# A two-layer attention and expert kernel: the projection bias of two row tiles is added in memory by accumulating transfers, and row loads, row sums and counts move

## The chip, the cores and the metric

The kernel runs on one core of one Trainium2 chip. The metric is the device time of one launch in microseconds (us), lower is better. Three runs of the kernel before gave 1204.27, 1204.51 and 1206.26 us; their median is 1204.51 us.

## The reference

The input x has 4 x 16 x 16 positions of 1024 channels, that is 1024 rows of 1024 float32 values. The kernel's tiles of rows are numbered 0 to 7, 128 rows each, two for each of the four images.

```python
# layer 0: group norm, q, k and v projections, content and position terms
x = x + _L0_conv_ref(_gn(x), Wq, Wk, Wv, ...)
# layer 1, attention: 16 heads of 64, causal, over 256 positions of each image
t = _to_tokens(x)
att = softmax(causal(q @ k.T / 8));  y = att @ v
t = t + (y @ W_proj.T + b_proj)
# layer 1, experts: 8 experts of 1024 x 1024, weights under 0.1 dropped
w = softmax(n @ gate_w + gate_b);  w = w * (w >= 0.1);  w = w / sum(w)
t = t + sum_e w[:, e] * (n @ expert_w[e] + expert_b[e])   # n = _ln_t(t)
```

What the change touches is `t + (... + b_proj)`: the rows after layer 0, the bias of the attention's output projection, and the product with `W_proj`. It also touches the bookkeeping of the experts: which rows have a weight of at least 0.1 for an expert, and how many such rows stand in the tiles before.

## The kernel before, in words

All work is on 128-row tiles in float32. A product of 128 x 1024 by 1024 x 512 is eight matmuls, which show as sixteen matmul records; many products are done as blocks by a Strassen-like scheme with seven products of four matmuls (eight records) each, whose operand sums are made on VectorE. `manual_schedule` blocks fix the order of the instructions of each engine as they are written; between two such blocks a scheduler merges what is ready.

**Layer 0** ends with a loop over the eight tiles (lines 636 to 660). The order of tiles is t = 1, 3, 5, 7, 0, 2, 4, 6. For the first six, GpSimd adds the broadcast bias `b_proj` to the rows (L647) and stores them to `x_rows` in memory (L656). The last two, t = 4 and t = 6, are stored by SyncE without the bias (L658 and L660).

**Attention** is a loop over d = 0 to 17 (L1028). In a step, TensorE does a few projection products (L682), multiplies the softmaxed scores of step d-2 with the values (L911, tile `pa`), and makes the scores of step d (L842). The scores of a step take a way through memory: `scored` scales them on GpSimd (L883), SyncE stores them (L889) and reads them back in four parts by quarters (L893, tile `s_rows`), and `turn_back` transposes them on VectorE (L898, tile `s_T`). There are two such sets, one after the other, in each step. SyncE works its queue in order, so a read back that waits holds up what is queued behind it. The weights of the next head pairs (`load_qk`, L785) are on that same queue at d = 0, 4 and 8.

From d = 13 the rows come back from memory. `load_x(t)` (L1051) is a 512 KB transfer on GpSimd's queue into `xs[t]`: t = 0 at d = 13, t = 1, 2 and 3 during d = 14, t = 4 and 6 in d = 15, t = 5 and 7 in d = 16. At the start of d = 15 the bias is loaded too, broadcast over 128 partitions (`bp`, L1084), and at d = 17 GpSimd adds it to tiles 4 and 6 (L1103). Tiles 2 and 3 (b = 1) are the first pair whose output projection goes by `product_out(1, n, ...)` (L964). `sum_of_weights(n)` (L947) makes its operand sums of the weights, `row_sums_out(b)` (L960) those of the rows. At the end of d = 16 `sum_of_weights(4)` stands ahead of `turn_back(17)`.

**The rest of the output projection** is a second `manual_schedule` block (L1545). TensorE does `product_out(1, 4)`, then the seven products of tiles 4 and 5 (b = 2, the second pair that goes by the seven-product scheme), then the full products of tiles 6 and 7. After each matmul `one_more` (L1538) counts one chunk, and the table `at_chunk` (L1487) says which stages of the gating are issued there, as pairs (stage, tile): 0 normalises a finished tile and stores it to `rows`, from where SyncE reads it back by quarters (L1276 and L182); 1 transposes it (L187); 2 is the product with the gate weights (L1325, tile `parts`); 3 and 4 are the softmax (`gate`) and the cut at 0.1 (`thresholds`); 5 counts rows per expert (`place`: L1380 adds the tile's kept flags to the running count `kept`, L1382 and L1383 turn flags and counts into positions on TensorE); 6 and 7 enter the rows into the experts' lists. Tiles 0 to 2 are gated together, and tiles 3 to 5. The table `others` (L1525) places single actions, among them `row_sums_out(2)` at chunk 12.

At chunk 8 tiles 0 and 1 are normalised; at chunk 12 tile 2 is normalised and then come the row sums of b = 2, so on VectorE the four sums (L160 to L163) stand behind the normalisation of tile 2. The transposes of tiles 0, 1 and 2 are issued at chunks 16, 20 and 26 and the product with the gate weights at chunk 30.

The experts' part (from L1588) takes the last 470 us and is not changed.

Of the kernel before, what the change touches and what calls it, by code (L numbers as in the profile page):

```python
# [32 lines left out]
F32 = mybir.dt.float32  # L33
I32 = mybir.dt.int32
AF = mybir.ActivationFunctionType
ALU = mybir.AluOpType
# [3 lines left out]
P = 128  # L40
C = 1024
# [4 lines left out]
NT = TOK // P  # L46
# [23 lines left out]
def kernel(  # L70
# [27 lines left out]
    nc = tc.nc  # L98

    def pool(stack, name, bufs=1, **kw):  # L100
        return stack.enter_context(tc.tile_pool(name=name, bufs=bufs, reuse_waits="tile", **kw))
# [49 lines left out]
    x_rows = dram.tile([TOK, C], F32, name="x_rows")  # L151
# [71 lines left out]
            nc.scalar.copy(dst[:, 4 * j : 4 * j + 4, ts(t, P)], pt.rearrange("p (c n) -> p c n", c=4))  # L223


    in_order, bp_home = ExitStack(), ExitStack()
    with ExitStack() as layer0:
        l0 = pool(layer0, "l0")
        xn = x_pool.tile([P, NC, TOK], F32, tag="x", name="xn")
# [434 lines left out]
    with ExitStack() as attention:  # L664
# [295 lines left out]
        def row_sums_out(b):  # L960
            a, s = rows_out_of(b)
            sums_of_A(*a, *s)
# [64 lines left out]
        with tc.manual_schedule():  # L1027
            for d in range(len(doubles) + lag):  # L1028
                if d % 4 == 0 and d < 12:
                    load_qk(d // 4 + 1)  # L1030
                elif d == 12:
                    w_p.append(w_tile("w_p0", W_projT[:, :HALF]))

                def values_and_scores(at):
                    if at >= lag:
                        values(at - lag, turned_s.pop(at - lag))
                    if at < len(doubles):
                        made[at] = scores(at)

                def go_on(at, between=lambda: None):  # L1040
                    if at - 1 in made:
                        first_one, second_one = made.pop(at - 1)
                        soft[at - 1] = [scored(*first_one)]
                        between()
                        soft[at - 1].append(scored(*second_one))

                def turn_back(at):
                    if at >= lag:
                        turned_s[at - lag] = [turned(*one) for one in soft.pop(at - lag)]

                def load_x(*some):  # L1051
                    for t in some:
                        nc.gpsimd.dma_start(xs[t], x_rows[ts(t, P), :])

                ahead = units.get(d, ())
                if d < 14:
                    for unit in ahead[:1]:
                        project_qk(*unit)
                    turn_back(d)
                    go_on(d)  # L1060
                    for unit in ahead[1:]:
                        project_qk(*unit)
                    if d == 13:
                        sums.close()
                        x_pool = pool(x_home, "xb", side="right")
                        xs = [x_pool.tile([P, C], F32, tag=f"x{t}", name=f"xb{t}") for t in range(NT)]
                        bp = pool(bp_home, "bp", side="right").tile([P, C], F32, tag="bp", name="bp")
                        load_x(0)
                    values_and_scores(d)
                elif d == 14:  # L1070
                    project_qk(*ahead[0])
                    go_on(14, lambda: load_x(1))
                    project_qk(*ahead[1])
                    turn_back(14)
                    w_p.append(w_tile("w_p1", W_projT[:, HALF:]))
                    sums_out.append(big_tile(1, "sums_out", (4 * Q, HALF)))
                    load_x(2)
                    project_out(*outs[14][0], {NC - 3: lambda: values_and_scores(14)}, True)
                    turn_back(15)
                    project_out(*outs[14][1], {}, True)  # L1080
                    go_on(15)
                    load_x(3)
                elif d == 15:
                    nc.gpsimd.dma_start(bp, b_proj.partition_broadcast(P))  # L1084
                    product_out(1, 1, tr)
                    product_out(1, 2, tr, {1: lambda: values_and_scores(15)})
                    sum_of_weights(1)
                    sum_of_weights(2)
                    project_out(*outs[15], {NC - 1: lambda: go_on(16)}, True)
                    row_sums_out(1)  # L1090
                    load_x(4, 6)
                    turn_back(16)
                elif d == 16:
                    project_out(*outs[16], {}, True)
                    load_x(5, 7)
                    product_out(1, 6, mm)
                    sum_of_weights(3)
                    product_out(1, 5, mm, {1: lambda: values_and_scores(16)})
                    sum_of_weights(4)
                    turn_back(17)  # L1100
                else:
                    for b, nt in tiles[NT - 2 :]:
                        nc.gpsimd.tensor_add(xs[2 * b + nt], xs[2 * b + nt], bp)  # L1103
                    product_out(1, 3, tr)
                    product_out(1, 7, tr, {1: lambda: values_and_scores(17)})
        share_banks("ps_rest", 3)
        bp_home.close()


    left.close()  # L1110
# [91 lines left out]
    with ExitStack() as gating:  # L1202
# [149 lines left out]
            nc.scalar.activation(weight, weight, AF.Exp)  # L1352
            return weight, top, keep

        def thresholds(weight, top, keep):
            n = top.shape[1]
            all_of = top.unsqueeze(2).to_broadcast([P, n, E])
            if n > 1:
                nc.vector.tensor_reduce(top, weight, AX.X, ALU.add)
            nc.vector.reciprocal(top, top)  # L1360
            if n == 1:
                of = weight[:, 0, :]
                nc.vector.tensor_scalar(keep[:, 0, :], of, top, THRESHOLD, ALU.mult, ALU.is_ge)
                nc.vector.scalar_tensor_tensor(of, of, top, keep[:, 0, :], ALU.mult, ALU.mult)
            else:
                nc.vector.tensor_mul(weight, weight, all_of)
                nc.vector.tensor_scalar(keep, weight, THRESHOLD, None, ALU.is_ge)
                nc.vector.tensor_mul(weight, weight, keep)
            nc.vector.tensor_reduce(top, weight, AX.X, ALU.add)
            nc.vector.scalar_tensor_tensor(top, top, 0.0, top, ALU.is_equal, ALU.add)  # L1370
            nc.vector.reciprocal(top, top)
            nc.vector.tensor_mul(weight, weight, all_of)
            return keep

        def place(tiles, keep):


            n, t0 = len(tiles), tiles[0]
            for i, t in enumerate(tiles):
                nc.vector.tensor_add(kept[:, t + 1, :], kept[:, t, :], keep[:, i, :])  # L1380
            pp = tr(f"pp{t0}")[:, : n * E]
            nc.tensor.matmul(pp, before, keep.rearrange("p n e -> p (n e)"), start=True, stop=False)  # L1382
            nc.tensor.matmul(  # L1383
                pp, ones, kept[:, t0 : t0 + n, :].rearrange("p n e -> p (n e)"), start=False, stop=True
            )
            slot = of_tiles("place", n, E)
            nc.vector.scalar_tensor_tensor(slot, keep, 0.0, from_end[:, t0 : t0 + n, :], ALU.is_equal, ALU.mult)
            at = l2w.tile([P, 3, n, E], I32, tag="at", name=f"at{t0}", padded_shape=[P, 3, 3, E])
            nc.vector.tensor_add(at[:, 0, :, :], slot, pp.rearrange("p (n e) -> p n e", n=n))
            nc.vector.tensor_scalar(at[:, 1, :, :], at[:, 0, :, :], 31, None, ALU.bitwise_and)  # L1390
            nc.vector.tensor_scalar(at[:, 2, :, :], at[:, 0, :, :], 5, None, ALU.logical_shift_right)
            return at
# [74 lines left out]
        def stage(n, t):  # L1467
            tiles = together[t]
            if n == 0:
                normal[t] = normalise(t)  # L1470
            elif n == 1:
                turned_rows[t] = turn_rows(t, normal[t])
            elif n == 2:
                summed[t] = gate_sums(tiles)
            elif n == 3:
                gated[t] = gate(tiles, summed[t])
            elif n == 4:
                gated[t] = thresholds(*gated[t])
            elif n == 5:
                placed[t] = place(tiles, gated[t])  # L1480
            elif n == 6:
                entered[t] = entries_of(t, t - tiles[0], placed[tiles[0]])
            else:
                enter(t, *entered[t])
# [16 lines left out]
            47: ((7, 1),),  # L1501
            48: ((1, 4),),
            50: ((7, 2),),
            53: ((1, 5),),
            55: ((2, 3),),
            57: ((0, 6),),
            58: ((3, 3),),
            59: ((4, 3),),
# [11 lines left out]
        def load_table(function):  # L1520
# [2 lines left out]
            nc.scalar.activation(of, ident[:, 0:1], function)  # L1523

        others = {  # L1525
            12: lambda: row_sums_out(2),
            29: lambda: nc.gpsimd.dma_start(
                w_p[1][:, : NC // 2, :], W_projT[:HALF, HALF:].rearrange("(c p) n -> p c n", p=P)
            ),
# [447 lines left out]
```

## Time and profile before

| | |
|---|---|
| median of three runs | 1204.51 us |
| the profiled execution | 1204.73 us |
| its span, first to last instruction | 1202.9 us |
| TensorE busy | 1191.1 us (99% of the span) |
| VectorE busy | 799.0 us (66%) |
| GpSimd busy | 416.2 us (35%) |
| ScalarE busy | 211.2 us (18%) |
| granted TensorE clock | 1.0 |

The span is the time from the first to the last instruction on the engines of the profiled execution; 1.8 us of the 1204.73 us lie around it. Times in the timelines count from the start of the span. A line of a timeline has the start, the duration (of a group: from its first start to its last end), the engine, the line in the kernel, the operation, what it writes and reads, shapes and how many; in square brackets how long the engine stood idle before it and what ended that. A line of the chain of waits has the start, the duration and the step that the work waited for. PE is TensorE, DVE VectorE, ACT ScalarE, POOL GpSimd and SPq SyncE's queue.

Attention runs from about 358 us to 650 us, the rest of the output projection to about 723 us, and the experts from there.

### The profile page before, as it was taken

The numbers are of one execution on the slowest core, as the hardware profiler recorded it, in microseconds if no ns is written. First come the engines' busy times: TensorE is split into PE (matmuls) and PEld (weight loads), VectorE is DVE, ScalarE is ACT, GpSimd is POOL, SyncE is SP. The second block draws the span as 40 slices with busy tenths as digits, with TensorE's granted clock in tenths as the row PEclk, the third lists the DMA queues.
The fourth block names the chain that finished last, engine by engine and source line by source line (L and its number), as shares of the span: only waits on it lengthen the run. The fifth ranks groups of instructions, "written<-read, shape, count | busy, mean of one in ns | idle before, by whom it ended". The sixth has DMA issues, their size and how long they took to land.

```text
span 1202.9 us, 13637 instructions
## 1 busy us (share of the span) xinstructions
PE 1191.1 (99%) x4866; PEld 649.3 (54%) x4866; DVE 799.0 (66%) x1394; ACT 211.2 (18%) x523; POOL 416.2 (35%) x470
## 2 busy tenths in 40 slices
PE   9999999999999999999999999999999999999998
PEld 5444884788884444444544464454344435444544
DVE  5796736678332666566679867897677767667852
ACT  3310111130001222122221212111111111111111
POOL 1051351365000122222333116546474554555411
PEclk9999999999999999999999999999999999999999
DMA  9102014882201353535565777484757475666434
GB/s 348 35 1 70 19 41 112 273 277 69 70 9 62 102 174 109 163 93 167 164 199 181 228 245 242 101 234 113 223 121 220 100 241 130 189 145 198 77 62 72
DMA packets 94330, 170.83 MB, mean 142 GB/s; under 512 B 12048, under 2 KB 49440, under 8 KB 94256
## 3 DMA queue, kind: packets, MB, share of 16 engines
q1 hardware_dynamic: 72880, 105.08, 26.6%
q0 software_dynamic: 16960, 54.59, 19.1%
q10 hardware_dynamic: 4416, 10.22, 2.4%
q8 instruction: 40, 0.66, 0.2%
q14 instruction: 34, 0.28, 0.1%
HBM read 117.17 MB, written 48.50 MB: 138 GB/s over the span
## 4 chain that ended last, share of the span: by engine, by line
PE 93%; DVE 3%; DMA 2%; issue 1%; SPq 0%; ACT 0%; POOL 0%; DVEq 0%; POOLq 0%
PE p L1662 27%; PE pqk L682 15%; PE pv L682 8%; PE joint L1724 4%; PE pq_pair L413 4%; PE pq L328 4%; PE left L1769 3%; PE po L1006 3%; PE pT L525 3%; PE py L617 2%; PE pk L444 2%; PE pc L465 2%; PE pv L553 2%; PE sc L842 2%; PE rest L1783 2%; PE pa L911 2%
## 5 line engine op out<-in xcount | busy, mean ns | idle before, releaser
L1145 POOL DMA_INDIRECT w_e_xg<-rows,gather x146 | 164.3, 1125 | 54.2 <-issue 42.4
L1662 PE MATMUL p<-w_e,A 128*128 128x512 f32 x368 | 162.1, 593 | 0.0
L883 POOL TENSOR_TENSOR s_q<-s_q,total 128x128 f32<-128x128 f32 (+1 forms) x128 | 61.8, 518 | 275.3 <-DVE total L880 264.4
L1662 PEld LDWEIGHTS p<-w_e,A 128*128 128x128 f32 x368 | 69.6, 190 | 86.8 <-issue 85.9
L1168 POOL DMA_INDIRECT out_dram<-y,add x32 | 58.7, 1834 | 163.6 <-issue 78.6
L1662 PE MATMUL p<-T,S 128*128 128x512 f32 x256 | 112.7, 592 | 0.0
L1711 ACT ACTIVATE y<-y,slot 128x512 f32<-128x512 f32 x64 | 45.4, 721 | 318.1 <-DVE y L1676 146.6
L682 PE MATMUL pqk<-ln,w_qk 128*128 128x512 f32 x192 | 85.7, 595 | 0.0
L1662 PEld LDWEIGHTS p<-T,S 128*128 128x128 f32 x256 | 48.6, 190 | 60.8 <-issue 60.3
L868 ACT ACTIVATE s_q<-sc,top 128x128 f32<-128x128 f32 (+1 forms) x128 | 52.0, 419 | 156.4 <-DVE top L864 137.8
L682 PEld LDWEIGHTS pqk<-ln,w_qk 128*128 128x128 f32 x192 | 36.1, 190 | 43.7 <-issue 42.1
L682 PE MATMUL pqk<-T,S_qk 128*128 128x512 f32 x128 | 57.8, 595 | 0.0
L1662 PE MATMUL p<-w_e,S 128*128 128x512 f32 x128 | 57.5, 592 | 0.0
L1006 PE MATMUL po<-w_p,y_T 128*128 128x512 f32 x112 | 50.7, 599 | 0.0
L328 PE MATMUL pq<-w_q,xn 128*128 128x512 f32 x96 | 44.5, 599 | 0.3 <-ACT xn L308 0.3
L682 PE MATMUL pv<-w_v,ln 128*128 128x256 f32 x192 | 43.2, 379 | 0.0
L1769 PE MATMUL left<-w_e,one 128*32 128x512 f32 x312 | 41.8, 593 | 0.0
L1662 PEld LDWEIGHTS p<-w_e,S 128*128 128x128 f32 x128 | 24.3, 190 | 30.6 <-issue 28.9
L898 DVE STREAM_TRANSPOSE s_T<-s_rows 128x768 f32<-128x768 f32 x32 | 30.2, 962 | 15.9 <-DMA s_rows<-s_rows 15.7
L187 DVE STREAM_TRANSPOSE A<-w_e_xg 128x1024 f32<-128x1024 f32 x32 | 39.5, 1235 | 1.4 <-DMA w_e_xg<-rows,gather 1.3
L682 PEld LDWEIGHTS pqk<-T,S_qk 128*128 128x128 f32 x128 | 24.0, 190 | 29.2 <-issue 27.7
L682 PEld LDWEIGHTS pv<-w_v,ln 128*128 128x128 f32 x192 | 36.4, 190 | 4.9
(388 smaller groups left out, 2056.0 us busy)
## 6 DMA issues: line engine op xcount, KB each, us to landing
w_e<-in_expert_w_dram SPq DMA_DIRECT2D x13, 2048.0 KB, 11.4
s_rows<-s_q SPq DMA_DIRECT2D x32, 384.0 KB, 2.3
s_rows<-s_rows SPq DMA_DIRECT2D x128, 96.0 KB, 2.4
w_qk<-in_W_attnT_dram SPq DMA_DIRECT2D x8, 1024.0 KB, 5.7
w_e<-in_expert_w_dram ACTq DMA_DIRECT2D x3, 2048.0 KB, 11.2
w_q<-in_Wq_dram SPq DMA_DIRECT2D x16, 256.0 KB, 6.8
x_at<-in_x_dram POOLq DMA_DIRECT2D x8, 512.0 KB
w_p<-in_W_projT_dram SPq DMA_DIRECT2D x2, 2048.0 KB, 8.3
```

Source lines behind the costliest of these rows:

```text
L328: nc.tensor.matmul(pq, xn[:, c, ts(t, P)], w_q[kc][:, c, :], start=(c == 0), stop=(c == NC - 1))
L413: nc.tensor.matmul(bank, a[:, c, :], b[:, c, :], start=(c == 0), stop=(c == NC // 2 - 1))
L682: nc.tensor.matmul(bank, stationary(c), moving(c), start=(c == 0), stop=(c == NC // 2 - 1))
L868: nc.scalar.activation(blocks(h, qt), psc[:, h, cols].rearrange("p (b f i) -> p b f i", f=Q, i=32), AF.Exp, bias=top[:, qt, h : h + 1], sc ...
L883: nc.gpsimd.tensor_mul(blocks(h, qt), blocks(h, qt), total[:, qt, h : h + 1].unsqueeze(2).unsqueeze(3).to_broadcast([P, 1 + qt, Q, 32]),)
L1006: nc.tensor.matmul(po, y_T[:, c, ts(t, P)], w_p[j][:, c, :], start=(c == 0), stop=(c == NC - 1))
L1145: nc.gpsimd.indirect_dma_start(out=row[:, g, :], out_offset=None, in_=table[: (TOK - P) * Q, :] if e in SHORT else table, in_offset=bass.I ...
L1168: nc.gpsimd.indirect_dma_start(out=out[: TOK - P, :] if e in SHORT else out, out_offset=bass.IndirectOffsetOnAxis(ap=add[:slots, e, k : k ...
L1662: nc.tensor.matmul(bank, a[:, c, :], b[:, c, :], start=(c == 0), stop=(c == NC // 2 - 1))
L1711: nc.scalar.mul(y, y, slot[:, e, 1, k : k + 1])
L1724: nc.tensor.matmul(of, a[:, c, :], b[:, c, :], start=(c == 0), stop=(c == NC // 4 - 1))
L1769: nc.tensor.matmul(bank[ts(i, 32), :], stationary, w[of][j][:, c, :], start=(c == 0), stop=(c == NC - 1))
```

## The change

1. `bp` as a tile of the attention's last steps goes, with its load at d = 15 and the two additions on GpSimd at d = 17. In their place stand two accumulating transfers on GpSimd's queue, at the start of d = 4 and of d = 5: the bias, broadcast over 128 rows, is added in memory to the rows of tile 4 and of tile 6 in `x_rows`.
2. Tile 4 is loaded at the end of d = 14, behind tile 3. Tiles 5, 6 and 7 are loaded at d = 17, on SyncE's queue. The four loads of d = 15 and d = 16 on GpSimd's queue go.
3. At the end of d = 16 `turn_back(17)` stands ahead of `sum_of_weights(4)`.
4. `row_sums_out(2)` moves from chunk 12 to chunk 10, so ahead of the normalisation of tile 2.
5. The additions to `kept` move from `place` into `thresholds`, right behind the line that makes the flags.
6. The transpose of tile 5 moves from chunk 53 to 54, and the gate product of tiles 3 to 5 from chunk 55 to 56.

```diff
                 ahead = units.get(d, ())
+                if d in (4, 5):
+                    b, nt = tiles[NT - 6 + d]
+                    nc.gpsimd.dma_start(
+                        x_rows[ts(2 * b + nt, P), :], b_proj.partition_broadcast(P), accum_op=ALU.add
+                    )
...
-                        bp = pool(bp_home, "bp", side="right").tile([P, C], F32, tag="bp", name="bp")
                         load_x(0)
...
                     go_on(15)
-                    load_x(3)
+                    load_x(3, 4)
                 elif d == 15:
-                    nc.gpsimd.dma_start(bp, b_proj.partition_broadcast(P))
                     product_out(1, 1, tr)
...
                     row_sums_out(1)
-                    load_x(4, 6)
                     turn_back(16)
                 elif d == 16:
                     project_out(*outs[16], {}, True)
-                    load_x(5, 7)
                     product_out(1, 6, mm)
                     sum_of_weights(3)
                     product_out(1, 5, mm, {1: lambda: values_and_scores(16)})
+                    turn_back(17)
                     sum_of_weights(4)
-                    turn_back(17)
                 else:
-                    for b, nt in tiles[NT - 2 :]:
-                        nc.gpsimd.tensor_add(xs[2 * b + nt], xs[2 * b + nt], bp)
+                    for t in (5, 6, 7):
+                        nc.sync.dma_start(xs[t], x_rows[ts(t, P), :])
                     product_out(1, 3, tr)
...
-        def thresholds(weight, top, keep):
-            n = top.shape[1]
+        def thresholds(tiles, weight, top, keep):
+            n = len(tiles)
...
                 nc.vector.tensor_scalar(keep[:, 0, :], of, top, THRESHOLD, ALU.mult, ALU.is_ge)
+                nc.vector.tensor_add(kept[:, tiles[0] + 1, :], kept[:, tiles[0], :], keep[:, 0, :])
...
                 nc.vector.tensor_scalar(keep, weight, THRESHOLD, None, ALU.is_ge)
+                for i, t in enumerate(tiles):
+                    nc.vector.tensor_add(kept[:, t + 1, :], kept[:, t, :], keep[:, i, :])
...
             n, t0 = len(tiles), tiles[0]
-            for i, t in enumerate(tiles):
-                nc.vector.tensor_add(kept[:, t + 1, :], kept[:, t, :], keep[:, i, :])
...
-            53: ((1, 5),),
-            55: ((2, 3),),
+            54: ((1, 5),),
+            56: ((2, 3),),
...
-            12: lambda: row_sums_out(2),
+            10: lambda: row_sums_out(2),
```

More of the change, by code (lines that the diff above doesn't have):

```diff
@@ L223, in turned_on_pe @@
             nc.scalar.copy(dst[:, 4 * j : 4 * j + 4, ts(t, P)], pt.rearrange("p (c n) -> p c n", c=4))
-    in_order, bp_home = ExitStack(), ExitStack()
+    in_order = ExitStack()
     with ExitStack() as layer0:
@@ L1106 @@
         share_banks("ps_rest", 3)
-        bp_home.close()
     left.close()
@@ L1477, in stage @@
             elif n == 4:
-                gated[t] = thresholds(*gated[t])
+                gated[t] = thresholds(tiles, *gated[t])
             elif n == 5:
```

## The prediction

> **What bounds the kernel now.** I read the page first, to see which engine sets the span.
>
> ```profile
> PE 1191.1 (99%) x4866; PEld 649.3 (54%) x4866; DVE 799.0 (66%) x1394; ACT 211.2 (18%) x523; POOL 416.2 (35%) x470
> ```
>
> TensorE is busy for 1191.1 of 1202.9 us. The change takes no matmul away, so it can only win what TensorE waits, 11.8 us in all. Next I asked the view of waits for TensorE's own.
>
> ```profile
> PE pa L911 <- DVE s_T L898: 2.1, 2, 1.8
> ...
> PE pp L1383 <- DVE kept L1380: 1.0, 1, 1.0
> ```
>
> The columns are the total, the times and the longest, in us. These two are the only TensorE waits of a microsecond that lie where the change works. The timeline shows the first, at d = 17:
>
> ```profile
> 631.68 2.16 POOL L1053 DMA_DIRECT2D xb<-x_rows  x4
> ...
> 636.38 5.10 POOL L1103 TENSOR_TENSOR xb<-xb,bp 128x1024 f32<-128x1024 f32 x2 [2.55 <-DMA xb<-x_rows]
> ...
> 639.20 4.43 DVE L952 TENSOR_TENSOR w_p<-w_p 128x2048 f32<-128x2048 f32 x1
> ...
> 645.54 2.28 DVE L952 TENSOR_TENSOR sums_out<-w_p,sums_out 128x2048 f32<-128x2048 f32 x1
> ...
> 647.74 1.82 DVE L898 STREAM_TRANSPOSE s_T<-s_rows 128x768 f32<-128x768 f32 x2
> ...
> 648.85 1.42 PE L911 MATMUL pa<-s_T,v 128*64 128x256 f32 x12 [1.85 <-DVE s_T L898]
> ```
>
> and the chain of waits shows what was late in memory:
>
> ```profile
> 634.05 8.85 DMA s_rows<-s_q
> ...
> 644.28 2.49 DMA s_rows<-s_rows
> ```
>
> The last scores' store took 8.85 us, where the page's median is 2.3: the four row loads, 2 MB, were issued 2 us ahead of it. So the scores are back at 646.8. By then VectorE is in `sum_of_weights(4)`, late itself, because `sum_of_weights(3)` took 4.43 us beside GpSimd's bias additions and not 2.28 as its twin does. The transposes start at 647.74 and TensorE stands for 1.85 us. The second wait is at chunk 40:
>
> ```profile
> 682.24 1.25 DVE L187 STREAM_TRANSPOSE row_T<-quarters 128x1024 f32<-128x1024 f32 x1
> 683.40 0.53 DVE L1380 TENSOR_TENSOR kept<-kept,g_keep 128x8 f32<-128x8 f32 x3
> ...
> 683.79 0.40 PE L1383 MATMUL pp<-kept,ones 128*128 128x24 f32 x2 [0.98 <-DVE kept L1380]
> ```
>
> The counts stand behind a normalisation and a transpose on VectorE.
>
> **Part by part: the bias and the loads.** Without the four loads the store at 634.05 should take about 3 us (637), the reads back 1.73 us of issuing and 2.4 of landing (641.2). VectorE without GpSimd beside it: L987 and L991 from 636.81 at 0.69 each (the same L991 later takes 0.69) to 638.2, the sum in 2.28 to 640.5, the values of d = 16 to 641.3, then it waits for TensorE's product that ends at 641.7 and evicts it (two of 0.67) until 643.0. Now `turn_back(17)` is next: 643.0 to 644.8, with scores that landed 1.8 us before. TensorE asks for them at 647.0. The wait of **1.85 us** goes with 2.2 us to spare. What stood ahead is late next: `sum_of_weights(4)` runs 644.8 to 647.1; its product starts at 650.4, so that costs nothing.
>
> The loads of tiles 5 to 7 are three issues of about 0.36 us on SyncE, behind the last L893 (about 639), and 1.5 MB behind the scores' reads on the same queue. Queued behind them on SyncE is only the read of row 0, issued at 655 before, so they are free; their data are first changed after 669. Tile 4's load takes the place of the bias load on GpSimd (0.54 us and 512 KB each) and is free too.
>
> The accumulating transfers: GpSimd issues one at about 427.1 and one at 442.7, behind its score work; its next work is at 438.9 and 454.0, so 0.6 to 1.8 us of issuing (plain load to indirect addition) hides. They have no row of their own. The nearest is the last indirect addition of 512 KB, issued at 1191.4, whose packets run from 1193.2 to 1197.2, 4 us with little beside it. At worst they hold up the scores for all of it. At d = 4 the second scores land at about 436.6, their transpose takes 0.98, and TensorE needs them halfway through its values, at 440.46 + 0.73: cover 3.6 us. At d = 5 it is 452.9 against 457.35 + 0.73: cover 4.2 us. Two holds of 4 us, partly carried over, cost between 0 and about 2 us; at d = 4 most of the store and read run beside the addition at a reduced rate, not stopped, so I take **0**.
>
> **The counts.** The three additions (0.53 us) now run right behind L1367, at about 678.3, 4 us before TensorE asks. That removes **0.98 us**. The work behind them on VectorE up to the transpose is 0.5 us later: the normalisation of tile 4 has cover, its row being transposed at 691.5 long before its product at chunk 56. With TensorE a microsecond earlier here the lists' entries of tile 0, ready on GpSimd at 687.0, are asked for at 687.5 and not 688.5: cover 0.5 us. Tile 5's transpose ended at 699.66 for a product that reached that tile at 699.73; moving both by one chunk (0.86 us) makes good for the 0.98 that TensorE gains, so this costs 0, with some 0.2 us of cover.
>
> **The row sums, the part that speaks against the change.** At chunk 10 the four sums (659.53 to 662.19, 2.66 us) pass ahead of the normalisation of tile 2:
>
> ```profile
> 657.25 1.28 DVE L1258 BATCH_NORM_STATS2 ln_stats<-xb 128x6 f32<-128x512 f32 x2
> ...
> 664.35 2.65 SPq L182 DMA_DIRECT2D quarters<-rows  x4
> ...
> 670.65 1.25 DVE L187 STREAM_TRANSPOSE row_T<-quarters 128x1024 f32<-128x1024 f32 x1 [0.38 <-DMA quarters<-rows]
> ...
> 671.70 1.52 PE L1325 MATMUL parts<-row_T,gw 128*32 128x128 f32 x48
> ```
>
> All of this starts when the values of d = 17 are done, so it moves 1.85 us earlier as a block. But row 2 loses 2.66 us of that and is stored (L1276, 660.92 before) at 661.73. The transpose then waits for memory, and TensorE wants row 2 after two thirds of its 1.52 us, at 671.70 - 1.85 + 0.97 = 670.82. Lightly loaded, a store takes 2.9 us until the read back is issued (row 5: 690.79 to 693.70), and the read 4.7 until the transpose (693.70 to 698.41): 661.73 + 2.9 + 4.7 + 1.25 = 670.6, a loss of 0. Heavily loaded they took 5.0 (row 3: 668.15 to 673.16) and 5.45 (row 1: 661.65 to 667.12): 673.4, a loss of 2.65 us. Row 2 will now be stored while row 1 is read back and 0.3 us ahead of tile 1's store to the output. The Trainium skill, DMA: Bandwidth & Descriptors, section Queues, rings and completion order, has each DMA engine take turns between the queues that have work. By that, row 2's store on ScalarE's queue need not wait for SyncE's reads: loss 0, total -2.83. The row of tile 3 says otherwise: its store, issued 1.05 us behind a store on SyncE's queue, took 5.0 and not 2.9 us; by it the total is -0.18. Here SyncE's other store comes after, so I go between but nearer to the light end: 3.6 for the store, 4.9 for the read, 671.5, a loss of **0.7 us**.
>
> The sums themselves are asked for by the product (2, 6) at about 660.7 and were ready before; their earlier place wins nothing.
>
> **The sum**: -1.85 - 0.98 + 0.7 = -2.13 us. From about 724 us TensorE is the bound again, and gathers and weight loads follow its progress, so the gain reaches the end. The profiled execution of 1204.73 (span 1202.9) would be 1202.6 (span 1200.8). It lies 0.2 us above the median of the runs, 1204.51, from which I forecast **1202.4 us**.
>
> **The rivals.** A measurement of this kernel tells about 0.2%, 2.4 us, from no change, so the bounds are 1202.1 and 1206.9. *Row 2 on time*: loss 0, 1204.51 - 2.83 = 1201.7, faster. For it: rows 4 and 5 came back in 7 to 8 us. Against it: at 655 to 672 the DMA engines are nearly full. *Row 2 as late as row 3's store says*: loss 1.3 to 2.65, 1203.0 to 1204.3; then the change does what it says at d = 17 and gives it back 20 us later. *Slower*: the accumulating transfers hold up the scores at d = 4 and 5 longer than their cover. With a hold of c each TensorE loses (c - 3.6) + (c - 4.2); against the gain of 2.13 it takes 2c - 7.8 = 4.53, so c = 6.2 us, for the end to be slower by 0.2%; at 8 us it is 1208.4. For it: the weights of the next pairs, 2 MB, are read from 434 on in the same queue as the scores, and each delay queues behind them. Against it: 4 us is what an addition took.
>
> **How the numbers follow.** Row 2 partly late (0.3 to 1.3 us lost) 0.45, a third of that below 1202.1; on time 0.28; heavily late 0.12; slower 0.15. Faster is 0.28 + 0.15 = 0.43, within 0.2% 0.30 + 0.12 = 0.42, slower 0.15. The range runs from 1201.2 (on time, and half a microsecond for the spread of runs) to 1205.0 (heavily late, and a part of the slower case), which leaves out some 0.15.
>
> **What the profile after would show.** Right: no TensorE wait at `pa` of d = 17 and none at L1383; the scores' last store at about 3 us; both L952 at 2.3 us. The transpose of row 2 waits 1 to 2 us for `quarters`, and TensorE waits some tenths for it at L1325. Wrong: a wait at L1325 over 1.3 us, or none; a wait at `pa` between 440 and 475; tile 5 late at chunk 56; or a VectorE order in which the sums don't delay row 2.

## The result, and the profile after

The changed kernel is **slower**. Its time is 1212.73 us (median of 6 runs, 1209.66 to 1214.13) against 1205.78 us for the kernel before on the same chip; the ratio is 1.0056, with a 95% interval of 1.0040 to 1.0071. The forecast was 1202.4 us, faster, with a range to 1205.0.

The profiled execution took 1212.29 us with a span of 1210.5, so 7.6 us more than the 1202.9 before. The page of the changed kernel has

```profile
span 1210.5 us, 13638 instructions
...
PE 1194.5 (99%) x4866; PEld 650.9 (54%) x4866; DVE 795.2 (66%) x1394; ACT 211.3 (17%) x523; POOL 410.8 (34%) x466
```

TensorE does the same 4866 records but is busy 3.4 us longer. No matmul was added, so some ran slower. The rest of the 7.6 us must be waiting. (L1325, L980 and the like are lines of the kernel that ran; an edit that adds lines shifts them.) The view of TensorE's waits of the changed kernel (total, times and longest, in us) shows where:

```profile
PE parts L1325 <- DVE row_T L187: 2.2, 1, 2.2
PE pa L911 <- DVE qk L820: 2.0, 1, 2.0
PE pa L911 <- DVE total L880: 2.0, 1, 2.0
...
PE po L980 <- DVE xb L996: 0.9, 1, 0.9
```

The two waits of before are gone: `pa` behind `s_T` at d = 17, and L1383 behind `kept`. The first line is row 2, which the prediction had with a smaller size. The next two are new: the values of d = 5 and of d = 4. These waits stand among what the prediction named as signs of being wrong (over 1.3 us at L1325; any at `pa` between 440 and 475).

**At d = 4 and 5.** The timeline of the changed kernel around the accumulating transfers (L1058):

```profile
427.04 0.87 POOL L1058 DMA_DIRECT2D x_rows<-in_b_proj_dram  x1
...
430.12 0.38 SPq L889 DMA_DIRECT2D s_rows<-s_q  x1
...
436.61 1.73 SPq L893 DMA_DIRECT2D s_rows<-s_rows  x4
...
438.43 1.02 SPq L129 DMA_DIRECT2D w_qk<-in_W_attnT_dram  x2
...
442.27 0.98 DVE L898 STREAM_TRANSPOSE s_T<-s_rows 128x768 f32<-128x768 f32 x1 [4.33 <-DMA s_rows<-s_rows]
...
443.31 0.97 PE L911 MATMUL pa<-s_T,v 128*64 128x256 f32 x8 [1.96 <-DVE total L880]
443.39 3.76 POOL L883 TENSOR_TENSOR s_q<-s_q,total 128x128 f32<-128x128 f32 x8 [15.48 <-DVE total L880]
...
444.21 2.93 PE L842 MATMUL sc<-qk 64*128 64x256 f32 x16
...
447.09 0.79 POOL L1058 DMA_DIRECT2D x_rows<-in_b_proj_dram  x1
...
450.87 0.38 SPq L889 DMA_DIRECT2D s_rows<-s_q  x1
...
457.74 1.73 SPq L893 DMA_DIRECT2D s_rows<-s_rows  x4
...
461.50 0.98 DVE L898 STREAM_TRANSPOSE s_T<-s_rows 128x768 f32<-128x768 f32 x1 [3.58 <-DMA s_rows<-s_rows]
...
462.51 0.66 DVE L820 TENSOR_TENSOR qk<-pqk,qk 128x512 f32<-128x512 f32 x1
...
463.23 1.72 PE L911 MATMUL pa<-s_T,v 128*64 128x256 f32 x16 [2.04 <-DVE qk L820]
```

and the same stretch of the kernel before:

```profile
429.51 0.38 SPq L889 DMA_DIRECT2D s_rows<-s_q  x1
432.46 1.73 SPq L893 DMA_DIRECT2D s_rows<-s_rows  x4
...
434.29 1.02 SPq L129 DMA_DIRECT2D w_qk<-in_W_attnT_dram  x2
...
438.93 3.75 POOL L883 TENSOR_TENSOR s_q<-s_q,total 128x128 f32<-128x128 f32 x8 [11.79 <-DVE total L880]
...
445.79 0.38 SPq L889 DMA_DIRECT2D s_rows<-s_q  x1
...
448.85 1.73 SPq L893 DMA_DIRECT2D s_rows<-s_rows  x4
...
452.91 0.98 DVE L898 STREAM_TRANSPOSE s_T<-s_rows 128x768 f32<-128x768 f32 x1 [4.26 <-DMA s_rows<-s_rows]
```

Read it as a chain. The store of the second scores (L889), which is in flight together with the addition, takes 430.12 to 436.61, so 6.5 us, where it took 429.51 to 432.46, 3.0 us. SyncE issues its queue in order: the reads back come 4.15 us later, and so do the weights behind them (L129, 438.43 and not 434.29). The last of the reads lands at 442.14, 4.24 us after its issue in the chain of waits; the median of such reads on the page of before is 2.4. That is 5.5 us later than the 436.6 from which the prediction counted its cover of 3.6. The second transpose of d = 4 starts at 442.27, and TensorE stands 1.96 us in the middle of the values. (The view names L880, the small instruction right behind that transpose on VectorE.)

At d = 5 the second scores are transposed at 461.50, 8.6 us later than before. Of these, 4.5 us are handed on by VectorE and GpSimd: L880 makes the reciprocals with which GpSimd scales the next scores, and it stands behind the blocked transpose, so L883 starts at 443.39 and not 438.93. The first store of d = 5 takes 0.6 us more than before, and the second, beside its own addition, 3.8 us more (450.87 to 457.74, where it took 445.79 to 448.85); the reads take 0.3 us less.

At d = 5 the waiting instruction isn't even the one that uses the scores. TensorE asks for `pa` and waits for L820, which empties an earlier product; on VectorE L820 stands behind the transpose that waits for memory. The cover of 4.2 us that the prediction counted, up to the second half of the values, is in truth shorter by this half (0.73) and by L820 (0.66): 2.8 us. TensorE comes to this place 3.8 us later than before itself, so the scores are 4.8 us late for it, 2.0 more than the cover.

Then there is the clock. The same 16 records of L842 take 2.93 us and not 1.58. A table of windows of the changed kernel (window, length, busy time of the engines, then TensorE's granted clock, the DMA engines' busy share and GB/s):

```profile
440.53:443.94 3.41, 1.45 (x17) 0.91 (x16) 1.67 (x5) 0.00 (x0) 0.55 (x2) 1.00 0.99 334
443.94:447.35 3.41, 3.41 (x23) 2.56 (x18) 3.27 (x7) 0.00 (x0) 3.41 (x8) 0.50 1.03 349
447.35:450.77 3.42, 3.42 (x9) 1.51 (x10) 2.27 (x6) 1.71 (x8) 0.53 (x1) 1.00 0.79 127
```

In the stretch with the wait TensorE is busy 1.45 of 3.41 us; for the next 3.41 us it is granted half its clock, which loses 1.7 us. The same follows the wait at d = 5, from 464.42 to 467.83. Together that is the 3.4 us of longer busy time.

**At d = 17** the timeline of the changed kernel is as forecast:

```profile
643.73 1.73 SPq L893 DMA_DIRECT2D s_rows<-s_rows  x4
...
645.51 2.28 DVE L952 TENSOR_TENSOR w_p<-w_p 128x2048 f32<-128x2048 f32 x1
...
650.46 1.83 DVE L898 STREAM_TRANSPOSE s_T<-s_rows 128x768 f32<-128x768 f32 x2
652.21 2.25 DVE L952 TENSOR_TENSOR sums_out<-w_p,sums_out 128x2048 f32<-128x2048 f32 x1
...
654.30 1.52 PE L911 MATMUL pa<-s_T,v 128*64 128x256 f32 x16
```

Both `sum_of_weights` take 2.3 us, the transposes come first, and `pa` has no wait in brackets.

**Row 2**, in the same timeline:

```profile
669.60 0.33 ACTq L1276 DMA_DIRECT2D rows<-row  x1
...
674.19 1.76 SPq L182 DMA_DIRECT2D quarters<-rows  x4
...
679.74 1.25 DVE L187 STREAM_TRANSPOSE row_T<-quarters 128x1024 f32<-128x1024 f32 x1 [3.05 <-DMA quarters<-rows]
...
681.04 0.65 PE L1325 MATMUL parts<-row_T,gw 128*32 128x128 f32 x16 [2.23 <-DVE row_T L187]
```

The store takes 4.6 us until its read is issued and the read 5.55 us until the transpose: nearly the heavy bounds of the prediction (5.0 and 5.45), not the 3.6 and 4.9 that it took.

The span's account: waits at d = 4 and 5 +4.0, two stretches at half clock +3.4, row 2 +2.2, the wait at L996 0.9 in place of 0.2, +0.7; the two waits that went -1.85 and -0.98. That is +7.5 of 7.6 us.

### The profile page after: what moved, and what is told of

Read it like the earlier page. It is cut to its first block, busy times and chain, and to the rows that moved or that the text cites. A ratio compares the mean times of both kernels' runs of the same rounds, so it can differ in the third digit from the quotient of the medians.

```text
span 1210.5 us, 13638 instructions
## 1 busy us (share of the span) xinstructions
PE 1194.5 (99%) x4866; PEld 650.9 (54%) x4866; DVE 795.2 (66%) x1394; ACT 211.3 (17%) x523; POOL 410.8 (34%) x466
## 4 chain that ended last, share of the span: by engine, by line
PE 92%; DMA 3%; DVE 2%; SPq 1%; issue 0%; ACT 0%; POOL 0%; DVEq 0%
PE p L1663 27%; PE pqk L682 14%; PE pv L682 8%; PE joint L1725 4%; PE pq_pair L413 4%; PE po L1006 4%; PE pq L328 3%; PE left L1770 3%; PE pT L525 3%; PE po L980 2%; PE py L617 2%; PE pk L444 2%; PE pc L465 2%; PE pv L553 2%; PE sc L842 2%; PE rest L1784 2%
## 5 line engine op out<-in xcount | busy, mean ns | idle before, releaser
L883 POOL TENSOR_TENSOR s_q<-s_q,total 128x128 f32<-128x128 f32 (+1 forms) x128 | 62.1, 521 | 281.0 <-DVE total L880 281.0
```

The lines of the kernel that those rows point to most:

```text
L883: nc.gpsimd.tensor_mul(blocks(h, qt), blocks(h, qt), total[:, qt, h : h + 1].unsqueeze(2).unsqueeze(3).to_broadcast([P, 1 + qt, Q, 32]),)
```

## The experiments

Three theories were open. **The addition**: the accumulating transfer holds up the scores' store, and the delay is handed on through SyncE's queue and VectorE's order. **Any transfer**: 512 KB more would do the same. **Other parts**: the wait for row 2 and the clock carry the loss. A ratio compares with runs of the kernel before on the same chip. It can differ from the quotient of the two medians: in experiment 5 it is 1.0033, or 4.0 us, while the medians differ by 2.9 us.

**1. The additions away from the scores.** They are issued right after the first weights' load, long before the attention's loop; all else is as in the changed kernel.

```diff
         load_qk(0)
+        for t in (4, 6):
+            nc.gpsimd.dma_start(x_rows[ts(t, P), :], b_proj.partition_broadcast(P), accum_op=ALU.add)
...
-                if d in (4, 5):
-                    b, nt = tiles[NT - 6 + d]
-                    nc.gpsimd.dma_start(
-                        x_rows[ts(2 * b + nt, P), :], b_proj.partition_broadcast(P), accum_op=ALU.add
-                    )
```

> The changed kernel with both accumulating transfers issued before the attention loop, where the queues and the DMA engines are nearly idle. Theory (the transfers hold up the scores at d = 4 and 5; each wait then halves the TensorE clock for 3.41 us): both waits at pa and both clock drops go, -4.0 -3.4 = -7.4 us against the changed kernel, about 1205. Rival (the row sums at chunk 10 are the main loser): it stays above 1209.

Measured: 1207.86 us, ratio 1.0016 (1.0008 to 1.0024). The waits at d = 4 and 5 are gone, so the place of the additions costs 0.4% of the time. It is slower than expected: the wait for row 2, 2.1 us, is followed by a stretch at half clock in this profile. Of the 20 runs, 7 have a mean clock of 0.997 or less and a median of 1209.9, the 6 at 0.999 or more 1205.9.

**2. The same, with the row sums back at chunk 12.**

```diff
-            10: lambda: row_sums_out(2),
+            12: lambda: row_sums_out(2),
```

> As the one before, and the row sums back at chunk 12. Theory (the row sums delay row 2 by 2.66 us, TensorE waits 2.2 us for it): another -2.2 us, about 1202.5 to 1203, and no wait at L1325. Rival (row 2 is late because the whole stage came 1.85 us earlier or because memory was full): the wait at L1325 stays over 1 us and the time is that of the run before within 1 us.

Measured: 1203.27 us (1202.41 to 1205.06), ratio 0.9983 (0.9973 to 0.9992). This version is faster than both kernels. Its waits:

```profile
PE po L982 <- DVE xb L998: 0.9, 1, 0.9
...
PE parts L1322 <- DVE row_T L187: 0.2, 1, 0.2
```

So the bias, the loads, the order at d = 17 and the counts together win 0.17%, or 2.0 us: -1.85 - 0.98 + 0.7 makes -2.1. The 0.7 is the first line, 0.9 us at L998 where before had 0.2: VectorE waits 1.03 us for a product ahead of the small set-up copies, which in the kernel before filled that time. All profiles of kernels with the edits at d = 17 have it at 0.9 us, the three built on the kernel before at 0.2. That the sum comes out like the forecast of -2.13 is chance: the forecast's 0.7 was for row 2.

**3 and 4. The kernel before, with only an addition or only a copy at d = 4 and 5.** The destination is a spare array in memory that nothing reads.

```diff
         load_qk(0)
+        spare = dram.tile([2 * P, C], F32, name="spare")
+        for i in range(2):
+            nc.gpsimd.dma_start(spare[ts(i, P), :], b_proj.partition_broadcast(P))
...
+                if d in (4, 5):
+                    nc.gpsimd.dma_start(
+                        spare[ts(d - 4, P), :], b_proj.partition_broadcast(P), accum_op=ALU.add
+                    )
```

The second kernel has a plain copy there, without `accum_op`.

> The kernel before with nothing but two accumulating transfers of 512 KB added at d = 4 and d = 5, into a spare part of memory that is filled before the loop. Theory: two waits of 2 us at pa and two windows at half clock, +7 us against the kernel before, about 1212. Rival (the loss comes with the other moves of the change): +0 to +1 us.

> As the one before, but the two transfers at d = 4 and d = 5 are plain copies of the same 512 KB, without accumulation. Theory (the accumulation's long packets hold up the scores): the hold is less than half, under the cover of 3.6 and 4.2 us, so 0 to +2 us. Rival (any 512 KB transfer at this place does it): +5 us or more.

Measured: with the additions 1211.03 us, 1.0043 (1.0026 to 1.0059), with the copies 1206.65 us, 1.0003 (0.9995 to 1.0012). The addition is the cause, and not the bytes: with the copies no wait at the values of d = 4 or 5 is listed. The view of DMA traffic from 424 to 460 us shows the difference; first with the additions (queue: packets, MB, share of 16 engines; then KB of each and median us to landing):

```profile
q0 software_dynamic: 288, 1.05, 20.7%
...
s_rows<-s_rows SPq DMA_DIRECT2D x16, 96.0 KB, 4.0
```

then with the copies:

```profile
q0 software_dynamic: 288, 1.05, 10.4%
...
s_rows<-s_rows SPq DMA_DIRECT2D x16, 96.0 KB, 2.9
```

The same 288 packets occupy the engines twice as long; 20.7% of 36 us for two additions is 3.7 us of all engines for each. With the additions TensorE's waits have

```profile
PE pa L914 <- DVE qk L823: 2.7, 1, 2.7
```

one wait at d = 5, with half clock after it, and not the two that were expected: at d = 4 the transpose came at 440.66, just in time. This execution's span is 6.1 us longer than that of before, of which 2.7 + 1.7 us are accounted for; the rest is open.

**5. The row sums alone.** The kernel before with `row_sums_out(2)` at chunk 10.

```diff
-            12: lambda: row_sums_out(2),
+            10: lambda: row_sums_out(2),
```

> The kernel before with one edit: the row sums of tiles 4 and 5 at chunk 10 and not 12. If the wait of 2.23 us for row 2 in the changed kernel comes from this alone: a wait of about 2.2 to 2.7 us at the gate product of tiles 0 to 2, and 1208 us (2.2 us more than before; 1.7 us more again if the idle time brings a stretch at half clock). If row 2 is late there only because the loads of tiles 5 to 7 now run on SyncE's queue beside it: no wait over 0.7 us and 1206 us.

Measured: 1208.68 us, 1.0033 (1.0023 to 1.0044).

```profile
PE parts L1325 <- DVE row_T L187: 2.4, 1, 2.4
PE pa L911 <- DVE s_T L898: 2.0, 2, 1.8
```

The wait is the row sums' own; the loads of tiles 5 to 7 on SyncE's queue have no part in it, since they aren't in this kernel. The profiled execution took 1207.43 us, 2.7 more than the one before, with the clock whole; of the 21 runs 8 have a mean clock of 0.997 or less and a median of 1211.7, the 9 at 0.999 or more 1207.4. The ratio's 4.0 us and the medians' 2.9 fit the wait of 2.4 and half clock in a part of the runs.

**6. The additions at d = 6 and 7**, where no weights are read beside them.

```diff
-                if d in (4, 5):
-                    b, nt = tiles[NT - 6 + d]
+                if d in (6, 7):
+                    b, nt = tiles[NT - 8 + d]
```

> The changed kernel with its accumulating transfers at the start of d = 6 and d = 7 in place of d = 4 and d = 5. No weights are read in these steps until 494 us, and the scores of the kernel before have 5 to 8 us in hand at TensorE there (transposed at 467.3 for 474.2, at 481.6 for 491.1). If the loss at d = 4 and 5 is the hold of the scores by the addition, made longer by the weights that are then read beside them: no wait at the values tile, no half clock at these steps, and some 7 us less than the changed kernel, 1205 to 1206 us. If an accumulating transfer takes that much from the core wherever it stands: about 1212 us again. By the landing of the second scores this also says what the addition alone delays: less than 5 us without the weights beside it, if these had a part in the 5.6 us of d = 4.

Measured: 1207.45 us, 1.0015 (1.0005 to 1.0026), the same as with the early additions, and 1.5 us or more above the figure expected. Row 2 waits 2.3 us, and here too the clock divides the runs: 7 of 22 at 0.997 or less have a median of 1210.2, the 8 at 0.999 or more 1206.2. No wait at the values of d = 6 or 7. The second transposes start at 469.36 and 486.86, and TensorE asks for these scores at 474.8 and 491.7: in these steps the hold is covered. It isn't smaller: the second stores take 6.4 us (459.13 to 465.49, 476.82 to 483.21) with no weights beside them, so the weights have no part in the store's 6.5 us at d = 4.

**7. Half of the bytes in each step**: 64 rows at each of d = 4, 5, 6 and 7.

```diff
-                if d in (4, 5):
-                    b, nt = tiles[NT - 6 + d]
-                    nc.gpsimd.dma_start(
-                        x_rows[ts(2 * b + nt, P), :], b_proj.partition_broadcast(P), accum_op=ALU.add
-                    )
+                if d in (4, 5, 6, 7):
+                    b, nt = tiles[NT - 2 + (d - 4) // 2]
+                    r = P * (2 * b + nt) + P // 2 * (d % 2)
+                    nc.gpsimd.dma_start(
+                        x_rows[r : r + P // 2, :], b_proj.partition_broadcast(P // 2), accum_op=ALU.add
+                    )
```

> The changed kernel with each accumulating transfer in two halves of 64 rows (256 KB), at the start of d = 4, 5, 6 and 7, so that each step has half of the bytes. If the hold of the scores goes with the bytes that are added: it halves to about 3 us at d = 4 (cover 3.6) and 3 to 4 us at d = 5 (cover 4.2), the waits at the values tile are under 0.5 us, the clock stays whole and the time is 1205 to 1207 us. If a fixed cost of an accumulating transfer holds the scores: waits of about 2 us remain at d = 4 and 5 and the time stays at 1211 to 1213 us.

Measured: 1206.89 us, 1.0015 (1.0005 to 1.0024). The hold goes with the bytes: the second transpose of d = 4 starts at 438.44, and at d = 5 there is

```profile
458.04 1.52 PE L911 MATMUL pa<-s_T,v 128*64 128x256 f32 x16 [0.47 <-DVE qk L820]
```

**8 and 9. Which of the two makes d = 5 late?** The additions at d = 4 and 6 (d = 5 comes after one), and at d = 5 and 7 (d = 5 has its own and none before). The edit of the first is shown; the second has 5 and 7 in it.

```diff
-                if d in (4, 5):
-                    b, nt = tiles[NT - 6 + d]
+                if d in (4, 6):
+                    b, nt = tiles[NT - 2 + (d == 6)]
```

> The changed kernel with its accumulating transfers at d = 4 and d = 6, so that d = 5 has none of its own but comes after one. At d = 4 the second scores' store takes 6.5 us and not 3.0, and the weights queue up behind it. If the wait at d = 5 comes mainly from what d = 4 hands on (the weights read 3.5 to 4 us later, beside the scores of d = 5): the second scores of d = 5 land some 4 us later than before (6 us with both transfers), and as 2.8 us are in hand there is a wait of about 1 us at the values tile of d = 5; the time is 1208 to 1210 us. If d = 5 is late only through its own transfer: no wait there and about 1207.5 us, as with the transfers at d = 6 and 7. If any one of the transfers before these scores brings 2 to 3 us and the half clock: 1211 us.

> The changed kernel with its accumulating transfers at d = 5 and d = 7, so that d = 5 has its own and nothing before it. If its own transfer alone holds the second scores by some 3.5 us (the store 6.5 and not 3.0): over the 2.8 us in hand by 0.7, so a wait of 0.7 us at the values tile of d = 5 and 1208 to 1209 us. If d = 5 is late only by what d = 4 hands on: no wait and 1207.5 us. If the transfer of d = 5 alone brings it: a wait of 2 to 3 us and 1210 to 1211 us.

Measured: at 5 and 7, 1206.55 us, 1.0015 (1.0007 to 1.0022); at 4 and 6, 1209.52 us, 1.0038 (1.0025 to 1.0052). The waits at d = 5, first with its own addition, then after the one of d = 4:

```profile
458.48 1.52 PE L911 MATMUL pa<-s_T,v 128*64 128x256 f32 x16 [0.81 <-DVE qk L820]
```

```profile
458.79 1.52 PE L911 MATMUL pa<-s_T,v 128*64 128x256 f32 x16 [0.39 <-DVE qk L820]
...
477.35 1.52 PE L911 MATMUL pa<-s_T,v 128*64 128x256 f32 x16 [1.60 <-DVE qk L831]
```

The own addition held the second store (445.59 to its read at 453.23, 7.6 us) 4.6 us longer than before, but the stores and reads around it were shorter: 0.8 us is about what was expected. The one of d = 4 hands on less than expected at d = 5: 3.2 us, if what this execution is late from its start is taken off. There the first scores' store takes 4.9 us (444.00 to 448.91) beside the late weights, and 3.1 before (440.85 to 443.94). Neither alone makes 2 to 3 us at d = 5; together they do. Unforeseen is the last line: after an addition at d = 4 the one of d = 6 does cost 1.6 us, though with additions at 6 and 7 it cost nothing. GpSimd issues it at 461.88 and not 456.36 (1.2 us of this from the start of the execution), behind score work that is itself late; the second store, issued at 464.59, is read back only at 470.96, 6.4 us later. A delay of the scores is handed on from step to step.

**10, 11 and 12. Is the half clock a consequence of the wait?** Work is put into the waits: the first two matmuls of the last projection product of d = 4 and 5 are done twice, or only the first; and the changed kernel once more beside the latter.

```diff
+            for c in range(again):
+                nc.tensor.matmul(bank, stationary(c), moving(c), start=(c == 0), stop=(c == again - 1))
...
-                        project_qk(*unit)
+                        project_qk(*unit, again=2 if d in (4, 5) and unit == ahead[-1] else 0)
```

> The changed kernel with the first two matmuls of the last projection product of d = 4 and of d = 5 done twice, so that TensorE has 0.86 us more to do in each of these steps (two matmuls at 0.43 us) while the scores come late. If the two stretches at half clock are a consequence of the idle time (1.96 and 2.04 us): the waits shrink to about 1.1 and 1.2 us by as much as was added, the clock stays whole, and 3.4 us come back, so about 1209.3 us. If the half clock has another cause, or a wait of 1.1 us brings it too: 1212.7 us as the changed kernel, since the added work fills time that was idle anyway. If the added work isn't hidden: 1214.4 us.

> The changed kernel with one matmul of the last projection product of d = 4 and of d = 5 done twice: two records of 0.43 us, so 0.86 us more for TensorE in each step, less than it waits there (1.96 and 2.04 us). If idle time of 2 us brings the stretch at half clock: waits of about 1.1 us, the mean granted clock of the runs at 0.998 to 0.999 where the changed kernel has 0.996, and some 2 to 3 us less than the changed kernel on the same chip, although it does more work. If the half clock has another cause or comes after 1.1 us as well: the time of the changed kernel, 1212 to 1213 us, at a clock of 0.996.

> The changed kernel once more, as the measure for the one before it: 1211 to 1213 us, two waits of about 2 us at the values tile of d = 4 and 5 and a clock of 0.996. If the delay of the scores differs from one execution to the next: waits that are shorter or longer than 1.96 and 2.04 us by some tenths, and runs at a clock of 0.998 or more where they are shorter.

Measured: two matmuls 1212.02 us, 1.0057 (1.0044 to 1.0070); one 1211.6 us, 1.0045 (1.0030 to 1.0059); the changed kernel again 1211.7 us, 1.0053 (1.0040 to 1.0066). The expectation of the first had a slip: a matmul shows as two records of 0.43 us, so two are 1.72 us and not 0.86; the one matmul is the intended dose. With two, no wait was left at the values of d = 4 and 5 (one of 0.8 us stood at d = 6), and no stretch ran at half clock. With one, there was none at d = 4 and 1.55 us at d = 5, and no half clock behind it; one stretch followed the wait for row 2. So the clock behaved as the theory says. The time did not: 0.1 us less than the changed kernel where 2 to 3 were expected, within the intervals of both. On the clock the fillers agree with the theory; on the time they decide nothing, since the scores' delay differs too much between executions: with two matmuls, the four runs at a mean clock of 0.999 or more still took 1209.8 to 1213.4 us. The repeat shows the difference:

```profile
PE pa L911 <- DVE qk L820: 3.2, 1, 3.2
PE parts L1325 <- DVE row_T L187: 2.4, 1, 2.4
```

Here the second transpose of d = 4 starts at 439.89 and not 442.27, d = 4 has no wait, and d = 5 has one of 3.2 with one stretch at half clock. The second scores of d = 5 came 6.0 us late against 2.8 in hand: 3.2 us. In both profiles the store at d = 4 took 6.5 to 6.6 us; what differs is the read behind it, 4.24 us in the chain of waits and 2.27 here. What decides that is open.

What all runs say of the clock: over the 155 runs of the changed kernel, its repeat and the eleven variants, each set against its own group's mean, 0.001 of mean clock goes with 1.16 us of time (correlation -0.75). 0.001 of 1207 us is 1.2 us, so a lower clock is enough to explain that part of the spread.

## Why the prediction was wrong

By the ratios the parts add up: -2.0 (experiment 2), +4.0 for the row sums (5), +5.2 for the additions (3), together +7.2 us; the changed kernel measured +6.8 and, in the repeat, +6.4. By the medians they fall short: -2.69 + 2.85 + 5.07 make 5.2, where 7.0 and 6.0 were measured. The intervals of the parts are 1.1 to 2.0 us to each side, so neither sum is a sharp test.

- **The bias, the loads and the order at d = 17: right.** The wait of 1.85 us went, the store fell to 2.6 us (forecast 3), both sums of weights to 2.3. The three loads on SyncE's queue cost nothing that shows: row 2 waits as long without them (experiment 5).
- **The counts: right.** The wait of 0.98 us is gone, with nothing late in its place at chunks 54 and 56.
- **The accumulating transfers, "I take 0": the step that failed.** They cost 4.0 us of waiting in one execution and 3.2 in the repeat, with stretches at half clock behind it. Three things were off.
  - *The hold.* 4 us "at worst" came from an indirect addition with little beside it, and one addition does hold the engines for about that long (3.7 us, experiment 3). But the second scores of d = 4 landed 5.5 us late in the first profile, over the cover of 3.6: that is the wait there. In the repeat it was 3.2 us, within the cover.
  - *What is handed on.* "Partly carried over" stood in the prediction, within its 0 to 2 us. In fact VectorE and GpSimd hand the delay on (L880 to L883), the late weights lengthen the next store (experiment 8), and at d = 5 the second addition comes on top: its second scores were 4.8 us late relative to TensorE in the first profile and 6.0 in the repeat.
  - *The cover.* 4.2 us was counted to the instruction that uses the scores, while L820, behind the blocked transpose on VectorE, needs that transpose to be over 1.4 us earlier. 4.8 and 6.0 less 2.8 are the waits of 2.0 and 3.2 us.

  The rival "slower" was right in kind and named the weights on the same queue, but it counted each step by itself. Its last figure is a slip: by its own formula a hold of 8 us makes 1202.4 + 8.2 = 1210.6 us and not 1208.4.
- **The clock: not in the sum at all.** A wait was counted at its length; some cost 1.7 us more, when the 3.41 us behind them ran at half clock.
- **The row sums, 0.7 us of 0 to 2.65: the term was mis-sized.** The order on VectorE was as forecast, and row 2's wait was 2.2 us, 2.4 in the kernel before with this edit alone. The rule of taking turns would have had 0 and the row of tile 3's store 2.65; the row was the better guide, and going between them towards the light end was the mistake. With the clock it is 4.0 us by the ratio of experiment 5.
- **A wait at L996 of 0.7 us more** came from the order in which set-up copies fall on VectorE, which I had not followed.

## What to carry to other kernels

Price a transfer that adds in memory by what else the DMA engines carry while it runs: here it held them twice as long as a copy, and a store beside it took 6.5 us in place of 3.0. Measure the cover of a late transfer to the first instruction queued behind the one that waits for it, on every in-order queue, and follow the delay into the next step. The additions are welcome where nothing waits for memory: issued before the attention's loop and with the row sums left at chunk 12, the same change wins 0.17%.

## What was not expected of the hardware

- **Half clock after about 2 us of idling.** The Trainium skill, TensorE: Matmul & The Clock Gate, Part 1, has TensorE at half clock after at least one idle window of 3413 ns that runs freely. The length and the free running fit. In the changed kernel the clock falls at 443.94, at 464.42 and, after the last matmul, at 1208.52 us; these are 6.00 and 218.00 times 3.413 us apart. In the seven other profiles that have such a stretch the fall at the end comes 155.0 or 218.0 times 3.413 us after it. So each execution has a fixed grid of 3.413 us. "Idle" doesn't fit: TensorE was busy for 1.45 and 1.37 of 3.41 us before the stretches (waits of 1.96 and 2.04 us), so no idle window was needed. By the page's words these waits would cost 4.0 us; measured, 7.4.

  The grid also explains why waits of one length differ. Cut along it, the nine windows ahead of the nine stretches have TensorE busy for 0.93 to 1.58 us. Of all other windows from 20 to 1195 us in the fourteen profiles the least busy has 1.57 us (the wait of 1.85 us of before); it kept the clock, as did all the others, from 1.63 us up. The wait of 2.1 us in experiment 1 falls whole into one window (busy 1.30 us); the 2.23 us for row 2 in the changed kernel are split between two (busy 2.76 and 1.83 us) and brought no stretch. So in these profiles the work in a window decides, near 1.6 of 3.41 us, and where a wait lies on the grid can cost or save 1.7 us.
- **An addition takes the DMA engines twice as long as a copy.** Experiments 3 and 4 show it: 20.7% and 10.4% for the same packets. Two windows, of the kernel before with the weights and of the changed kernel with the second addition, look alike to the busy share and not to the rate:

```profile
438.00:440.00 2.00, 2.00 (x6) 0.76 (x4) 2.00 (x5) 0.00 (x0) 1.07 (x3) 1.00 1.09 354
```

```profile
450.00:452.00 2.00, 2.00 (x6) 0.82 (x5) 0.00 (x0) 0.78 (x4) 0.00 (x0) 1.00 1.04 169
```

The engines are full in both (shares of 1.09 and 1.04), at 354 and 169 GB/s. Not all of this is the addition's: scores are stored and read in the second window too, and that traffic by itself can fill the engines at a low rate (kernel before, 460 to 461 us: a share of 0.99 at 192 GB/s).
